# Soft mixture-of-experts layer: the combination's steps pinned a tile apart, column variances, single turn pieces, two tiles combined early

## The chip, the cores and the metric

The kernel runs on one core of one Trainium2 chip. A core has five engines that run beside each other, each with its own instruction queue: TensorE (PE, matrix products and transposes into PSUM banks), VectorE (DVE), ScalarE (ACT), GpSimd (POOL) and SyncE (SP, which here issues nearly all DMAs). The metric is the device time of one execution in microseconds (us); lower is better. All values are float32 unless a trace line says otherwise.

## The reference

The input is 4096 rows of 256 values. Four residual blocks follow each other, each behind a LayerNorm:

```
x = x + attention_a(layernorm(x))      # 16 heads of 16, causal, softmax with an extra term in its sum
x = x + softmoe(layernorm(x))
x = x + attention_b(layernorm(x))      # 16 heads of 16, causal
x = x + softmoe(layernorm(x))
```

The change is in the soft mixture of experts, which is (64 experts of 32 slots, so 2048 columns):

```
logits  = (x @ phi_w.T + phi_b).reshape(4096, 64, 32)
D       = softmax(logits, over the 32 slots)
C       = softmax(logits, over the 64 experts)
Xt      = D^T x                         # 2048 x 256: every slot's mixture of the rows
Xt      = tanh(layernorm(clip(Xt, -33000, 65000)))
Yt      = Xt[expert] @ expert_w[expert] + expert_b[expert]
out     = C Yt                          # 4096 x 256
```

## The kernel before

Rows are cut into 32 tiles of 128 (`NT`), and `x` stays in SBUF. The program runs attention a, the first expert layer, attention b and the second expert layer. An expert layer (`_Experts.run`) has three sweeps over the 32 tiles and a transition.

**First and second sweep** (`h` = 0 and 1: the first and the second 1024 of the 2048 columns). `logits(h, t)` makes 128×1024 logits on PE (tile `lg`), adds the bias on DVE (L775), stores the result to a DRAM tile `ld[t]` for later, takes the maximum per expert on DVE (L780), subtracts it on POOL (L783), takes the exponential on ACT (L786), and keeps the maximum over experts in `cm` (L787, DVE). `divide(h, t)` sums on DVE (L796), inverts (L797) and multiplies on POOL (L798): that is D. PE then adds Dᵀx into four PSUM banks `acc` (four calls of 512 columns per tile). Logits run two tiles ahead of the accumulation, and division one tile ahead.

**Pieces beside.** `net.side` is a queue of small pieces; `net.beside(3)` takes one. After each accumulation two are taken in the first sweep and one in the second. In the first sweep the pieces come from `norm_pieces`: row statistics, scaling, and two turns for every four tiles. A turn transposes two tiles of `x` on PE (L70) into the `bank` of the pool `psm`, which holds one bank, and ACT copies it to `xnT` (L753). The first eight tiles are normed and turned ahead of the sweep. In the second sweep the pieces are the LayerNorm of the first half of X̃ (which stands transposed, features in partitions) and its expert products: `centre` (mean by a matmul with a constant matrix, subtraction on DVE, square on POOL L693), `spread` (variance by a matmul with the same matrix, so repeated over all 128 partitions; square root on ACT L701; reciprocal of 128×512 on DVE L702), `squash` (multiplication on POOL L707, tanh on ACT L708), and eight `product`s (PE, then a bias add on DVE L720).

**Transition.** The second half of X̃ goes through the same steps. Between them stand the first tile's turn and the first half of its combination. Combination of tiles 0 and 1 begins at the end of the second sweep.

**Third sweep** (the combination, C Ỹ). `combine_begin(t)` loads the 128×2048 logits (1 MB) and the residual rows `xl`, takes `mc`, the larger of the two halves' `cm`, on DVE (L811), subtracts it on POOL in two halves (L815) and takes exponentials on ACT (L818). `combine_sums(t)` reduces over the experts on DVE (L824), inverts (L825) and repeats the 32 sums four times by a POOL copy, `s4` (L827). `turn(t)` transposes that to `rT` on PE, copies it to `r` on ACT (L835), makes 16 transposes of 128×128 in groups of four into `ps` (four PSUM banks), and multiplies each group by `r` into `lT` on DVE (L842). `weigh(t)` is 16 matmuls into `o` and a residual add on DVE (L860); in the first layer row statistics follow (`net.stats`, L94 and L95), in the second the store. Step `t` of the loop writes `combine_begin(t+2)`, `turn(t+1)`, `combine_sums(t+2)` and `weigh(t)`. In the first layer, the first pieces of attention b are taken in this loop from tile 6 on.

**The order.** A tile scheduler orders each engine's instructions by its own costs. Exempt are those under `keep_in_program_order`, which stay in the order they are written: before, that holds for PE's matmuls and transposes alone (`net.mm`, L66, and `net.tr`, L69). Where a pool has fewer buffers than the program has open tiles of it, the next write waits for the last reader.

Of the kernel before, what the change touches and what calls it, by code (L numbers as in the profile page):

```python
# [19 lines left out]
P = 128  # L20
# [586 lines left out]
class _Experts:  # L607
# [8 lines left out]
    def __init__(self, net, phiT, phi_b, ew, eb, out=None, attention=None):  # L616
        self.net, self.phiT, self.phi_b = net, phiT, phi_b
        self.ew, self.eb, self.out = ew, eb, out
        self.attention = attention
        self.phi = net.zone[:, 0 : 2 * E].rearrange("p (c e) -> p c e", c=2)  # L620
        self.phb = net.zone[:, 2 * E : 3 * E]

    def load(self):
        nc, EH = self.net.nc, E // 2
        for h in range(2):
            for c in range(2):
                nc.sync.dma_start(
                    self.phi[:, c, ts(h, EH)], self.phiT[ts(c, P), ts(h, EH)]
                )
# [5 lines left out]
    def run(self):  # L635
# [10 lines left out]
        with ExitStack() as ctx:  # L646
# [4 lines left out]
            sp = pool("ff_s", 4)  # L651
            net.banks = pool("psm", 1, space=PSUM)
# [3 lines left out]
            nc.gpsimd.memset(mean, 1.0 / D)  # L656
            ys = [cp.tile([P, NC2, D], F32, name="ys0"), None]
# [8 lines left out]

            def load_w(ec, w=None):
                if w is None:
                    w = ewp.tile([P, 4, 2, D], F32, name="w")
                nc.sync.dma_start(w, ew[ts(ec, 4)].rearrange("n (c p) h -> p n c h", p=P))  # L670
                ews[ec] = w

            def load_b(h):
                b = rp.tile([P, NC2, D], F32, name="ebt")
                for j in range(4):
                    nc.sync.dma_start(
# [5 lines left out]

            sqs = {}

            def centre(n):
# [4 lines left out]
                sq = ewk.tile([P, 2, 512], F32, name="sq")  # L690
                for d in range(2):
                    nc.vector.tensor_tensor(xs[:, d, :], xs[:, d, :], mu, ALU.subtract)
                    nc.gpsimd.tensor_tensor(sq[:, d, :], xs[:, d, :], xs[:, d, :], ALU.mult)  # L693
                sqs[n] = sq

            def spread(n):
                sq = sqs[n]
                var = net.bank()
                for d in range(2):
                    mm(var, mean, sq[:, d, :], start=d == 0, stop=d == 1)  # L700
                nc.scalar.activation(sq[:, 0, :], var, AF.Sqrt, bias=net.eps)  # L701
                nc.vector.reciprocal(sq[:, 0, :], sq[:, 0, :])  # L702

            def squash(n):
                xs = xt[:, :, ts(n, 512)]
                for d in range(2):
                    nc.gpsimd.tensor_tensor(xs[:, d, :], xs[:, d, :], sqs[n][:, 0, :], ALU.mult)  # L707
                nc.scalar.activation(xs, xs, AF.Tanh)  # L708

            def product(ec):  # L710
                w = ews.pop(ec)
                y = net.bank()[:, 0:D]
# [20 lines left out]
            def norm_pieces(j):  # L733
                def stats(i2):
                    for t in (4 * j + 2 * i2, 4 * j + 2 * i2 + 1):
                        net.stats(t)
                    if i2:
                        net.roots(4 * j, 4 * j + 4)

                def scale():  # L740
                    for t in range(4 * j, 4 * j + 4):
                        nc.scalar.activation(
                            x[:, t, :], x[:, t, :], AF.Identity,
                            bias=shift[:, t : t + 1], scale=rstd[:, t : t + 1],
                        )

                def turn(i2):
                    t2 = 2 * j + i2
                    pt = net.bank().rearrange("p (c i t) -> p c i t", c=2, i=2)
                    for i in range(2):  # L750
                        for c in range(2):
                            tr(pt[:, c, i, :], x[:, 2 * t2 + i, ts(c, P)])
                    nc.scalar.copy(  # L753
                        xnT[:, :, ts(t2, 2 * P)], pt.rearrange("p c i t -> p c (i t)")
                    )

                return [
                    lambda: stats(0), lambda: stats(1), scale, lambda: None,
                    lambda: turn(0), lambda: turn(1),
                ]  # L760
# [4 lines left out]
            def logits(h, t):  # L765
                l = lp.tile([P, NH, SLOT], F32, name="l")
                lf = l.rearrange("p n s -> p (n s)")
                for n in range(2):
                    lg = pl.tile([P, 512], F32, name="lg")
                    for c in range(2):  # L770
                        mm(
                            lg, xnT[:, c, ts(t, P)], phi[:, c, ds(h * EH + n * 512, 512)],
# [5 lines left out]
                nc.sync.dma_start(ld[t][:, h, :], lf)  # L778
# [22 lines left out]
            ce, css, lTs, xls, pools = {}, {}, {}, {}, {}  # L801

            def combine_begin(t):
                l = pools["l"].tile([P, NEXP, SLOT], F32, name="l")
                nc.sync.dma_start(
                    l.rearrange("p n s -> p (n s)"), ld[t].rearrange("p h e -> p (h e)")
                )
                xl = sp.tile([P, D], F32, name="xl")
                nc.sync.dma_start(xl, xd[:, t, :])
                m = sp.tile([P, SLOT], F32, name="mc")  # L810
                nc.vector.tensor_tensor(m, cm[:, t, 0, :], cm[:, t, 1, :], ALU.max)  # L811
                e = pools["e"].tile([P, NEXP, SLOT], F32, name="e")
                for h in range(2):
                    ns = ts(h, NH)
                    nc.gpsimd.tensor_tensor(  # L815
                        e[:, ns, :], l[:, ns, :], _bc(m.unsqueeze(1), [P, NH, SLOT]), ALU.subtract
                    )
                    nc.scalar.activation(e[:, ns, :], e[:, ns, :], AF.Exp)  # L818
                ce[t], xls[t] = e, xl


            def combine_sums(t):
                s = sp.tile([P, SLOT], F32, name="sc")
                nc.vector.tensor_reduce(s, ce[t].rearrange("p n s -> p s n"), AX.X, ALU.add)  # L824
                nc.vector.reciprocal(s, s)  # L825
# [241 lines left out]
```

## Time and profile before

| | us |
|---|---|
| three runs | 5325.7, 5330.68, 5327.17 |
| median | 5327.17 |
| the profiled execution | 5322.71 |
| its span, first to last instruction | 5321.0 |
| first layer: first sweep, second sweep | 276.4, 241.8 |
| first layer: transition, third sweep (tiles 2 to 31) | 75.0, 297.8 |
| second layer: first sweep, second sweep | 276.5, 242.2 |
| second layer: transition, third sweep (tiles 2 to 31) | 74.9, 295.3 |

| engine | busy us | share of the span |
|---|---|---|
| PE | 5025.3 | 94% |
| DVE | 4142.4 | 78% |
| ACT | 2608.9 | 49% |
| POOL | 1208.7 | 23% |

The stages were cut by the trace: a sweep runs from its first logits or transposes to the end of its last accumulation, the transition from there to the first matmul of `weigh(2)`. In the lines of a trace, `o<-ys,lT` names the output tile and the inputs of an instruction, `128*128 128x512` the contraction and the output of a matmul; a float32 matmul appears as several records. `[9.59 <-POOL s L827]` behind an instruction is the idle time of its engine before it and what ended it. In the rows by group the columns are busy time, mean nanoseconds of one, and idle time with its releasers. PEclk is the granted TensorE clock, 1.00 being full speed; PE's busy time is partly modelled.

### The profile page before, as it was taken

How to read it: one execution, taken by the hardware profiler on the slowest of the kernel's cores; microseconds unless marked ns; L12 is line 12 of the kernel's file. 1: busy time of each engine (PE TensorE's matmuls, PEld its weight loads, DVE VectorE, ACT ScalarE, POOL GpSimd, SP SyncE). 2: the span in 40 equal slices, each digit the busy share in tenths (PEclk: the TensorE clock that was granted, in tenths of full speed). 3: DMA queues.
4: the chain of work that ended last, by engine and by line, in shares of the span. 5: the costliest groups of instructions: out<-in, count | busy, mean ns of one | idle time of the engine just before them, and what ended most of it. 6: DMA issues, size and time to landing. Idle time of an engine off the chain costs nothing.

```text
span 5321.0 us, 79263 instructions
## 1 busy us (share of the span) xinstructions
PE 5025.3 (94%) x29824; PEld 2663.5 (50%) x29824; DVE 4142.4 (78%) x7742; ACT 2608.9 (49%) x3036; POOL 1208.7 (23%) x1178
## 2 busy tenths in 40 slices
PE   7999999999999899979989999999999998999799
PEld 4444454545454344447744454444454543444577
DVE  5788998989987478767757888989899864787665
ACT  3566666666677412122235666666666674111221
POOL 3211000000000345454411110000000003455443
PEclk9999999999999999989989999999999999999899
DMA  6433221222211211443353342222222112113432
GB/s 248 140 111 121 74 68 63 69 63 63 62 59 42 85 68 67 138 142 113 119 199 130 105 128 68 66 70 61 63 63 67 56 36 86 67 75 135 143 129 90
DMA packets 265584, 499.16 MB, mean 94 GB/s; under 512 B 44880, under 2 KB 109904, under 8 KB 257008
## 3 DMA queue, kind: packets, MB, share of 16 engines
q1 hardware_dynamic: 259968, 485.57, 27.5%
q10 hardware_dynamic: 4896, 7.87, 0.4%
q8 instruction: 234, 3.83, 0.3%
q14 instruction: 150, 1.23, 0.1%
q0 software_dynamic: 336, 0.66, 0.0%
HBM read 336.73 MB, written 156.76 MB: 93 GB/s over the span
## 4 chain that ended last, share of the span: by engine, by line
PE 65%; DVE 14%; POOL 11%; ACT 4%; issue 4%; DMA 1%; SPq 0%; DVEq 0%; POOLq 0%; ACTq 0%
PE bank L67 20%; PE o L67 20%; PE sc L67 17%; POOL e L815 5%; DVE mx L386 4%; DVE sc L824 4%; PE lg L67 3%; POOL e L783 3%; PE acc L67 3%; DVE junk L380 2%; POOL e L798 2%; ACT e L786 2%; DVE l L775 1%; ACT e L818 1%; ACT pb L462 1%
## 5 line engine op out<-in xcount | busy, mean ns | idle before, releaser
L462 ACT ACTIVATE pb<-sc 128x1024 f32<-128x1024 f32 (+3 forms) x2304 | 2071.0, 951 | 1093.2 <-PE sc L67 1090.3
L386 DVE TENSOR_REDUCE mx<-bank 128x1 f32<-128x512 f32 x3584 | 2223.2, 681 | 169.9 <-PE bank L67 165.7
L67 PE MATMUL bank<-k,q 64*128 64x512 f32 (+3 forms) x4608 | 1350.0, 452 | 72.8 <-DVE mx L386 29.9
L67 PEld LDWEIGHTS bank<-k,q 64*128 64x128 f32 x4608 | 666.5, 185 | 1178.6 <-DVE mx L386 780.3
L67 PE MATMUL o<-pb,va 128*32 128x512 f32 (+3 forms) x9216 | 1158.2, 574 | 0.9 <-POOL pb L466 0.7
L67 PE MATMUL sc<-q,k 64*128 64x512 f32 (+3 forms) x4608 | 988.1, 390 | 9.9 <-ACT pb L462 9.4
L67 PE MATMUL sc<-qm,one 64*128 64x512 f32 (+3 forms) x4608 | 946.9, 376 | 0.0
L466 POOL TENSOR_SCALAR_AFFINE_SELECT pb<-pb 128x256 f32<-128x256 f32 x512 | 205.7, 408 | 2260.5 <-ACT pb L462 2254.8
L380 DVE CUSTOM_DVE_ANT_0 junk<-bank,maskw 128x128 bf16<-128x128 f32 (+3 forms) x1024 | 501.6, 490 | 259.1 <-PE bank L67 151.8
L67 PEld LDWEIGHTS sc<-q,k 64*128 64x128 f32 x4608 | 508.8, 186 | 138.4 <-ACT pb L462 99.8
L67 PEld LDWEIGHTS sc<-qm,one 64*128 64x128 f32 x4608 | 525.6, 186 | 66.6
L786 ACT ACTIVATE e<-e 128x1024 f32<-128x1024 f32 x128 | 135.2, 1056 | 786.3 <-POOL e L783 786.3
L67 PE MATMUL acc<-e,x 128*128 128x512 f32 x1024 | 472.1, 605 | 35.2 <-POOL e L798 33.6
L67 PE MATMUL lg<-zone,xnT 128*128 128x512 f32 x1024 | 469.3, 602 | 0.2
L67 PE MATMUL o<-ys,lT 128*128 128x256 f32 x2048 | 453.0, 379 | 0.0
L67 PEld LDWEIGHTS o<-ys,lT 128*128 128x128 f32 x2048 | 384.5, 190 | 51.8 <-issue 2.0
L818 ACT ACTIVATE e<-e 128x1024 f32<-128x1024 f32 x128 | 135.3, 1057 | 459.3 <-POOL e L815 449.6
L67 PEld LDWEIGHTS acc<-e,x 128*128 128x128 f32 x1024 | 197.9, 194 | 290.5 <-issue 242.4
L798 POOL TENSOR_TENSOR e<-e,s 128x1024 f32<-128x1024 f32 x128 | 244.7, 1913 | 385.7 <-DVE s L797 385.7
L67 PEld LDWEIGHTS o<-pb,va 128*32 128x32 f32 x9216 | 182.9, 108 | 285.8 <-issue 263.2
L67 PEld LDWEIGHTS lg<-zone,xnT 128*128 128x128 f32 x1024 | 194.9, 193 | 242.5 <-issue 229.5
L815 POOL TENSOR_TENSOR e<-l,mc 128x1024 f32<-128x1024 f32 x128 | 299.6, 2363 | 24.1 <-DVE x L860 17.1
(101 smaller groups left out, 3234.9 us busy)
## 6 DMA issues: line engine op xcount, KB each, us to landing
k<-ak SPq DMA_DIRECT2D x144, 512.0 KB
k<-bk SPq DMA_DIRECT2D x144, 512.0 KB
ld<-l SPq DMA_DIRECT2D x128, 512.0 KB
l<-ld SPq DMA_DIRECT2D x64, 1024.0 KB
w<-in_L_ffn_expert_w_dram SPq DMA_DIRECT2D x24, 1024.0 KB
q<-aq SPq DMA_DIRECT2D x32, 512.0 KB
rb<-dd SPq DMA_DIRECT2D x64, 256.0 KB
q<-bq SPq DMA_DIRECT2D x32, 512.0 KB
```

The costliest lines, as they stand in the source:

```text
L67: self.tc.keep_in_program_order(self.nc.tensor.matmul(*a, **k))
L380: nc.vector.tensor_tensor_reduce(out=junk[:, 0:w], in0=scs[h2][:, 0:w], in1=maskw[:, QB - w : QB], scale=1.0, scalar=-3e38, op0=ALU.add, o ...
L386: nc.vector.tensor_reduce(m, scs[h2], AX.X, ALU.max)
L462: nc.scalar.activation(pb[:, :, off:QB], sc[:, :, off:QB], AF.Exp)
L466: nc.gpsimd.affine_select(out=d, in_=d, compare_op=ALU.is_ge, fill=0.0, base=0, pattern=[[0, 2], [1, P]], channel_multiplier=-1,)
L775: nc.vector.tensor_tensor(lf[:, ts(n, 512)], lg, phb[:, ds(h * EH + n * 512, 512)], ALU.add)
L783: nc.gpsimd.tensor_tensor(e, l, _bc(m.unsqueeze(2), [P, NH, SLOT]), ALU.subtract)
L786: nc.scalar.activation(ef, ef, AF.Exp)
L798: nc.gpsimd.tensor_tensor(e, e, _bc(s.unsqueeze(2), [P, NH, SLOT]), ALU.mult)
L815: nc.gpsimd.tensor_tensor(e[:, ns, :], l[:, ns, :], _bc(m.unsqueeze(1), [P, NH, SLOT]), ALU.subtract)
L818: nc.scalar.activation(e[:, ns, :], e[:, ns, :], AF.Exp)
L824: nc.vector.tensor_reduce(s, ce[t].rearrange("p n s -> p s n"), AX.X, ALU.add)
```

## The change

- `phi` is laid out with the halves of the columns outermost, so that each half lies together in the zone; tile 0's early exponentials and the last loads of weights are written over the parts no longer read.
- Every DMA of the layer on SP is pinned to its written order (`dma`), and the DVE and ACT steps of the combination too (`pin`).
- `centre` squares on ACT in one operation. `spread` makes the variances as columns: eight one-column matmuls, root and reciprocal of 128×4, and a product of the identity with them on DVE. `squash` turns that diagonal back to rows by one matmul with ones, and multiplies on DVE from PSUM.
- The norm of a group of four tiles is one piece (`norm`), and each turn is a piece of its own (`turn_x`). The first two turns are written to `lg` banks. In the first sweep one piece is taken before the accumulation and one after it; in the second, one before it.
- The combination is split: `maxima`, `load_l`, `begin`, `sums` (or `quarter` four times), `turn_r`, `turn`, `weigh`, `ended`. In step `t` of the third sweep stand `load_l(t+4)`, `ended(t-1)`, `begin(t+3)`, `turn(t+1)`, `maxima(t+4)`, `sums(t+2)`, `weigh(t)`, `turn_r(t+2)`. The copy `s4` is on ACT. `ps` has three banks, and products of the transition alternate between two.
- Tiles 0 and 1 begin in the second sweep: subtractions and exponentials by halves at steps 14, 16, 18 and 20, sums by quarters at 21 to 28, and their turns ahead of the last two accumulations. Tile 2 begins there too, and its sums are taken by quarters between the transition's products.
- Attention b's first pieces start one tile later (6 and 10 instead of 5 and 9).

The diff, cut to its core:

```diff
+        self.phi = net.zone[:, 0 : 2 * E].rearrange("p (h c e) -> p h c e", h=2, c=2)
...
+            pin = tc.keep_in_program_order
+            def dma(o, i):
+                pin(nc.sync.dma_start(o, i))
...
-                sq = ewk.tile([P, 2, 512], F32, name="sq")
                 for d in range(2):
                     nc.vector.tensor_tensor(xs[:, d, :], xs[:, d, :], mu, ALU.subtract)
-                    nc.gpsimd.tensor_tensor(sq[:, d, :], xs[:, d, :], xs[:, d, :], ALU.mult)
-                sqs[n] = sq
+                sqs[n] = ewk.tile([P, 2, 512], F32, name="sq")
+                nc.scalar.activation(sqs[n], xs, AF.Square)
             def spread(n):
                 sq = sqs[n]
                 var = net.bank()
-                for d in range(2):
-                    mm(var, mean, sq[:, d, :], start=d == 0, stop=d == 1)
-                nc.scalar.activation(sq[:, 0, :], var, AF.Sqrt, bias=net.eps)
-                nc.vector.reciprocal(sq[:, 0, :], sq[:, 0, :])
+                for k in range(4):
+                    for d in range(2):
+                        mm(
+                            var[:, k : k + 1], sq[:, d, ts(k, P)], mean[:, 0:1],
+                            start=d == 0, stop=d == 1,
+                        )
+                r = sp.tile([P, 4], F32, name="rx")
+                nc.scalar.activation(r, var[:, 0:4], AF.Sqrt, bias=net.eps)
+                nc.vector.reciprocal(r, r)
+                nc.vector.tensor_tensor(
+                    sq[:, 0, :].rearrange("p (k e) -> p k e", k=4),
+                    _bc(net.ident.unsqueeze(1), [P, 4, P]), _bc(r.unsqueeze(2), [P, 4, P]),
+                    ALU.mult,
+                )
             def squash(n):
                 xs = xt[:, :, ts(n, 512)]
+                rs = net.bank()
+                mm(rs, one, sqs[n][:, 0, :], start=True, stop=True)
                 for d in range(2):
-                    nc.gpsimd.tensor_tensor(xs[:, d, :], xs[:, d, :], sqs[n][:, 0, :], ALU.mult)
+                    nc.vector.tensor_tensor(xs[:, d, :], xs[:, d, :], rs, ALU.mult)
                 nc.scalar.activation(xs, xs, AF.Tanh)
...
+            def maxima(t):
+                cms[t] = sp.tile([P, SLOT], F32, name="mc")
+                pin(nc.vector.tensor_tensor(cms[t], cm[:, t, 0, :], cm[:, t, 1, :], ALU.max))
+            def load_l(t):
+                cl[t] = pools["l"].tile([P, NEXP, SLOT], F32, name="l")
+                dma(cl[t].rearrange("p n s -> p (n s)"), ld[t].rearrange("p h e -> p (h e)"))
+                xls[t] = xlp.tile([P, D], F32, name="xl")
+                dma(xls[t], xd[:, t, :])
+            def exponentials(t, l, h):
+                ns, e = ts(h, NH), ce[t]
+                nc.gpsimd.tensor_tensor(
+                    e[:, ns, :], l, _bc(cms[t].unsqueeze(1), [P, NH, SLOT]), ALU.subtract
                 )
...
+                pin(nc.scalar.activation(e[:, ns, :], e[:, ns, :], AF.Exp))
+            def begin(t):
+                ce[t] = pools["e"].tile([P, NEXP, SLOT], F32, name="e")
+                l = cl.pop(t)
                 for h in range(2):
...
+                    exponentials(t, l[:, ts(h, NH), :], h)
+            def inverse(t, s):
+                pin(nc.vector.reciprocal(s, s))
+                css[t] = sp.tile([P, 4, SLOT], F32, name="s4")
+                pin(nc.scalar.copy(css[t], _bc(s.unsqueeze(1), [P, 4, SLOT])))
+            def sums(t):
                 s = sp.tile([P, SLOT], F32, name="sc")
...
+                pin(nc.vector.tensor_reduce(
+                    s, ce[t].rearrange("p n s -> p s n"), AX.X, ALU.add
+                ))
+                inverse(t, s)
+            sqp = {}
+            def quarter(t, k):
+                if k == 0:
+                    sqp[t] = sp.tile([P, 4, SLOT], F32, name="sq4", bufs=2)
+                pin(nc.vector.tensor_reduce(
+                    sqp[t][:, k, :], ce[t][:, ts(k, NEXP // 4), :].rearrange("p n s -> p s n"),
+                    AX.X, ALU.add,
+                ))
+                if k == 3:
+                    s = sp.tile([P, SLOT], F32, name="sc")
+                    pin(nc.vector.tensor_reduce(
+                        s, sqp.pop(t).rearrange("p k s -> p s k"), AX.X, ALU.add
+                    ))
+                    inverse(t, s)
+            def turn_r(t, bank=None):
+                rT = (bank or (lambda: pools["r"].tile([P, 512], F32, name="rT")))()[:, 0:P]
                 tr(rT, css.pop(t).rearrange("p j s -> p (j s)"))
...
+                rts[t] = sp.tile([P, P], F32, name="r")
+                pin(nc.scalar.copy(rts[t], rT))
+            def turn(t, bank=None):
+                r = rts.pop(t)
                 e = ce.pop(t).rearrange("p n s -> p (n s)")
                 lT = pools["lT"].tile([P, NEC, P], F32, name="lT")
                 for e4 in range(NEC // 4):
...
+                    ps = (bank or (lambda: pools["t"].tile([P, 512], F32, name="ps")))()
+                    ps = ps.rearrange("p (i t) -> p i t", i=4)
                     for i in range(4):
                         tr(ps[:, i, :], e[:, ts(4 * e4 + i, P)])
...
+                    pin(nc.vector.tensor_tensor(
                         lT[:, ts(e4, 4), :], ps, _bc(r.unsqueeze(1), [P, 4, P]), ALU.mult
...
+                    ))
                 lTs[t] = lT
...
+            def ended(t):
+                pin(nc.vector.tensor_tensor(x[:, t, :], os.pop(t), xls.pop(t), ALU.add))
...
+            first = lambda: pl.tile([P, 512], F32, name="lg")
+            norm(0)
+            norm(1)
+            turn_x(0, first)
+            turn_x(1, first)
+            for j in range(2, NT // 2):
+                if j % 2 == 0 and j > 2:
+                    net.side.append(lambda j=j: norm(j // 2))
+                net.side.append(lambda j=j: turn_x(j))
             seq = [(h, t) for h in range(2) for t in range(NT)]
...
+            def early(t, h):
+                if h == 0:
+                    maxima(t)
+                    ce[t] = z(0, E) if t == 0 else rp.tile(
+                        [P, NC2, D], F32, name="ebt"
+                    ).rearrange("p c (n s) -> p (c n) s", s=SLOT)
+                    xls[t] = xlp.tile([P, D], F32, name="xl")
+                    dma(xls[t], xd[:, t, :])
+                l = z(2 * E, EH)
+                dma(l.rearrange("p n s -> p (n s)"), ld[t][:, h, :])
+                exponentials(t, l, h)
+            ahead = {}
+            for k in range(4):
+                ahead[14 + 2 * k] = lambda k=k: early(k // 2, k % 2)
+            for k in range(8):
+                ahead[21 + k] = lambda k=k: quarter(k // 4, k % 4)
+            ahead[29] = lambda: [maxima(t) for t in range(2, 4)]
...
+                if n < len(seq) - 2:
+                    net.beside(3)
+                else:
+                    assert not net.side and not net.urgent and not net.agenda
+                if h == 1 and t in ahead:
+                    ahead[t]()
                 if n == len(seq) - 2:
                     nctx.close()
-                    pools["e"] = pool("fc_w", 2)
+                    pools["lT"] = pool("fc_t", 2)
                     pools["l"] = pool("fc_l", 1)
-                    pools["lT"] = pool("fc_t", 1)
+                    pools["e"] = pool("fc_w", 1)
+                    load_l(2)
+                    turn_r(0, first)
+                    turn(0, first)
+                    begin(2)
...
+                    load_l(3)
+                if n == len(seq) - 1:
+                    turn_r(1, first)
+                    turn(1, first)
+                    load_b(1)
...
+                if h == 0:
+                    net.beside(3)
...
+            pools["e"] = pool("fc_w1", 1)
             pools["r"] = pool("fc_r", 1, space=PSUM)
-            pools["t"] = pool("fc_p", 4, space=PSUM)
+            pools["t"] = pool("fc_p", 3, space=PSUM)
             pools["o"] = pool("fc_o", 2, space=PSUM)
+            two = pool("fc_x", 1, space=PSUM)
+            weigh(0, 0, NC2)
             centre(2)
             centre(3)
-            turn(0)
             spread(2)
             spread(3)
-            weigh(0, 0, NC2)
+            weigh(1, 0, NC2)
             squash(2)
             squash(3)
             for ec in range(NC2, NEC):
-                product(ec)
-                if ec == NC2:
-                    load_w(NEC - 1)
+                product(ec, (net.bank, lambda: two.tile([P, 512], F32, name="bank2"))[ec % 2])
+                if ec < NC2 + 2:
+                    load_w(ec + 6)
+                if ec < NC2 + 4:
+                    quarter(2, ec - NC2)
+            turn_r(2)
+            begin(3)
...
             for t in range(NT):
-                if t + 2 < NT:
-                    combine_begin(t + 2)
+                if t + 4 < NT:
+                    load_l(t + 4)
+                if t > 0:
+                    ended(t - 1)
+                    if t + 3 < NT:
+                        begin(t + 3)
                 if t == 0:
                     weigh(0, NC2, NEC)
-                if t + 1 < NT:
+                if 2 <= t + 1 < NT:
                     turn(t + 1)
-                if t + 2 < NT:
-                    combine_sums(t + 2)
+                if t > 0 and out is None:
+                    net.stats(t - 1)
+                if t + 4 < NT:
+                    maxima(t + 4)
+                if 4 <= t + 2 < NT:
+                    sums(t + 2)
                 if t > 0:
-                    weigh(t, 0, NEC)
+                    weigh(t, NC2 if t == 1 else 0, NEC)
+                if 4 <= t + 2 < NT:
+                    turn_r(t + 2)
+                if t == 0:
+                    sums(3)
+                    turn_r(3)
...
-                    if t in (5, 9):
-                        b = (t - 5) // 4
+                    if t in (6, 10):
+                        b = (t - 6) // 4
...
-                    if t > 5:
+                    if t > 6:
                         net.beside(3)
+            ended(NT - 1)
```

## The prediction

> **What bounds the kernel now.** I read the chain first, for the engine at the end of the work.
>
> ```profile
> PE 65%; DVE 14%; POOL 11%; ACT 4%; issue 4%; DMA 1%; SPq 0%; DVEq 0%; POOLq 0%; ACTq 0%
> ```
>
> The attention sections (all before 1780 us and 2671 to 4428 us) issue the same instructions in both kernels, so I cut the rest into stages: busy times for each layer's first sweep, second sweep, transition (last accumulation to `weigh(2)`) and third sweep.
>
> ```profile
> core 0: us, PE busy (x) PEld busy (x) DVE busy (x) ACT busy (x) POOL busy (x), PEclk, DMA share, GB/s
> 1780.20:2056.60 276.40, 252.39 (x624) 115.49 (x623) 201.99 (x223) 50.14 (x58) 131.71 (x80) 0.98 0.24 88
> 2056.60:2298.40 241.80, 229.65 (x628) 98.81 (x627) 187.21 (x201) 40.32 (x38) 124.77 (x69) 0.98 0.36 125
> 2298.40:2373.40 75.00, 42.74 (x278) 29.90 (x276) 46.23 (x44) 19.81 (x22) 39.47 (x25) 0.84 0.37 125
> 2373.40:2671.20 297.80, 284.82 (x1475) 236.81 (x1474) 212.40 (x294) 74.96 (x104) 128.96 (x80) 1.00 0.34 116
> ...
> 4947.20:5022.10 74.90, 42.80 (x277) 29.96 (x277) 45.79 (x43) 19.81 (x22) 37.97 (x24) 0.84 0.33 114
> 5022.10:5317.40 295.30, 276.19 (x1438) 230.40 (x1436) 189.89 (x224) 59.49 (x80) 128.83 (x80) 1.00 0.33 113
> ```
>
> First-layer sweeps leave PE idle 24 and 12 us; the transition 32, at a clock of 0.84. The third sweep looks PE-bound, but busy PE there is partly a modelled wait. Its chain shows the real period:
>
> ```profile
> 5102.46 3.71 DVE sc L824
> ...
> 5106.20 0.36 DVE sc L825
> ...
> 5106.68 0.05 POOL s L827
> ...
> 5106.93 4.69 POOL e L815 x2
> ...
> 5111.64 1.06 ACT e L818
> ...
> 5112.73 3.71 DVE sc L824
> ```
>
> This repeats every 10.27 us: POOL's small copy L827 queues between one tile's subtractions and the next's, so subtractions, exponentials and sums of neighbouring tiles cannot overlap. At the end, where tiles are ready in advance, outputs come 8.76 to 8.80 us apart (6.91 for `weigh`, 1.86 for the turn): PE's own need.
>
> **First sweep.** Both turns of a pair use the one `bank`, so the second waits for ACT's copy, which stands behind an exponential:
>
> ```profile
> L70 PE MATMUL bank<-ident,x 128*128 128x128 f32 x128 | 21.2, 290 | 32.0 <-ACT xnT L753 32.0
> ```
>
> The change puts the turns in separate pieces and the first two in other banks: −16 per layer. One more saved at the start (5.1 us of transposes and copies through one bank). Two attention-output projections that stood together are now apart: −2.5 (the second waited 2.47). Against this, POOL's loop through subtraction, exponential, sum and multiply takes 7.125 us where PE needs 6.87; PE's stalls hid that. Over some 20 tiles 0.255 each shows: +5. Sum −14; bounds −18 (POOL's pace hidden) and −8 (half of the turn waits return as waits for the copy).
>
> **Second sweep, norm of X̃.** The slow steps are these (transition rows; the sweep's own are alike):
>
> ```profile
> L702 DVE RECIPROCAL sq<-sq 128x512 f32<-128x512 f32 x2 | 6.5, 3293 | 0.0
> L707 POOL TENSOR_TENSOR xt<-xt,sq 128x512 f32<-128x512 f32 x4 | 5.0, 1265 | 3.7 <-DVE sq L702 3.7
> ```
>
> Two 3.3-us reciprocals and four POOL multiplies delay POOL's normal multiply, and the accumulations stand 14.06 and 10.49 us apart where 6.87 would do. With variances as columns the reciprocal has 4 columns (L825 with 32 takes 0.35), the diagonal is one DVE multiply of 512 elements (at most 0.7), the way back one 0.85-us matmul, and the scaling four DVE operations of 0.68 (as L692). The square's one ACT operation of 1024 elements costs 1.06, off the path. The fourteen steps that carry these pieces and the products now take 8.58 + 8.85 + 8.79 + 8.58 + 7.66 + 14.06 + 10.49 + 7×8.08 = 124; I get 2×8.58 + 2×8.7 + 2×7.7 + 8×8.09 + 3 of stalls left = 118: −6, between 0 and −9.
>
> **Second sweep, early tiles.** Subtractions and exponentials of tiles 0 and 1 fit in POOL's 3.3-us idle stretch between subtraction and multiply, so they cost about 1. The quarter sums do not: 3.71/4 = 0.93 of DVE stands between reciprocal and second logit add, on the 7.125 loop. With 0.26 of slack used up already, eight cost some 0.83 each: 6.6, and two closing sums and reciprocals with the maxima 1.2: +8.8. Reloading `l` by halves is SP work with free bandwidth (DMA share 0.36); bounds: 3 (DVE's slack absorbs most) to 14 (each early piece costs its whole duration). Turns of tiles 0 and 1 before the last two accumulations add 3.7 of PE time, partly under waits of 2.17 and 2.96 there: +3.4. Sweep net: −6 + 8.8 + 3.4 ≈ +6, from −2 to +14.
>
> **Transition.** Before, 75. Now PE has: means 3.4, first halves of `weigh(0)` and `weigh(1)` 6.9, variances 3.6, broadcasts 1.7, products 8×1.3 = 10.4 (two banks; 1.67 each now), second halves 6.9, turn(2) and two small ones 2.5: 35.4. Uncovered: clips of the last sums 2.8; scaling, table load (1.28) and tanh to the first product 6; the copy of r behind an exponential before `turn_r(3)` 3.5; pool changes 1.5. Together 49.2: −26, bounds −30 and −15 (the square, sqrt and reciprocal in a row, still uncovered, are the low bound's).
>
> Here the clock matters. In before, PE resumes after `[9.59 <-POOL s L827]` and 16 transposes take 3.4 us, where the chain's steady 16 take 1.75. The Trainium skill ("TensorE: Matmul & The Clock Gate", HAM oscillation) says that idle stretches beyond about 3.4 us bring the slow clock back; by it my 6 and 3.5 would each still cost some 2 us, and the transition would be 53. I keep 49: my stretches are bounded above by less than the 9.59 seen.
>
> **Third sweep.** Now the copy `s4` goes to ACT, subtractions run a tile ahead (`begin(t+3)` beside `weigh(t)`), sums of t+2 and turns of t+1 follow in a pinned order. POOL needs 4.7 a tile, ACT 2×1.06 + 2×0.3, DVE x 0.36, lT 4×0.62 (0.68 with the pipeline's start), mc 0.19, sc 3.71, reciprocal 0.36: 7.1 to 7.4. PE's 8.77 is the bound. What is queued behind each wait: with three `ps` banks instead of four, the turn's last four transposes wait for the first lT, which waits for `ended(t-1)`'s add: about 0.23. So 9.0 × 30 = 270 in the second layer against 295.3: −25 (bounds −27 and −5).
>
> In the first layer ACT, in about eight tiles by the built order, copies r only behind the next tile's two exponentials, and in some five separate places PE then waits 1.9 to 2.6: +12. Attention pieces make eight tiles longer: 22×9.13 + 4×9.5 + 4×10.5 = 281. One more piece is left over after the last tile: +2.4. Sum 295.4 against 297.8: −2 (bounds −14 and +12).
>
> **Sum.** 2×(−14 + 6 − 26) − 25 − 2 = −95. The profiled execution took 5322.71 at a span of 5321.0; span 5226, execution 5228. It lies 4.5 under the median of 5327.17, so the forecast is 5232. A measurement of this kernel can tell about 0.2%, 10.7 us, from no change (its three runs spread over 5).
>
> **Rivals.**
> Cleaner (0.13): the r copies never come late, the first layer's third sweep gains like the second's (−15 to −25), early work is absorbed: −120, 5207. For: ACT is 25% busy there. Against: the built order.
>
> The third sweep keeps its period (0.14). The row
>
> ```profile
> L811 DVE TENSOR_TENSOR mc<-cm 128x32 f32<-128x32 f32 x19 | 3.7, 193 | 46.3 <-POOL e L815 46.3
> ```
>
> shows mc starting only when both subtractions of POOL have ended, 2.43 later than it could. The change pins mc(t+4) ahead of the sums of t+2. If mc waits for POOL itself, and not for a buffer's last reader, DVE's tile becomes 7.3 + 2.4 = 9.75: 30 tiles 293, about −2 in the second layer and nothing in the first. Then the sweeps' −68 are all: 5257. Against: the lT multiplies, with one SBUF input, show no such wait. The Trainium skill ("SBUF — State Buffer", Who interferes with whom) speaks for it: a DVE instruction with two SBUF inputs is locked out while a GpSimd one reads SBUF. The waits of 2.43 agree, though a buffer's release would look alike; by that rule the time is this rival's 5257.
>
> Slower: lockstep on the fourth turn bank (0.09). With three banks PE stands until DVE frees the first. If DVE is then still inside its 3.71 reduction, PE waits it out in every tile: 8.77 + 3.7 = 12.5, 375 per third sweep, +157 for both, less 68: +89, 5416. It decides where DVE's 7.1 to 7.4 of a tile, begun when `weigh(t-1)` ends, are not done as `weigh(t)` ends, 8.77 later. Slack is 1.4, less what hand-offs take, and statistics of the first layer (0.4) come out of it; I see no more than 0.5 of hand-offs in the chain above, which speaks against.
>
> The change does not do what it says (0.04): turns still share one bank after the first two, and if ACT's copies stay behind exponentials, all stage gains fall to their low bounds: 2×(−8 + 14 − 15) = −18, and the third sweeps 0 with the extra 2.4 and 12 of the first layer: −4, no change.
>
> **How the numbers follow.** The forecast has 0.60. Faster: 0.60 + 0.13 (cleaner) + 0.14 (period kept) = 0.87; same 0.04; slower 0.09. The range starts at 5195, below the cleaner rival's 5207, since the sweeps' upper bounds would take another 12, and ends at 5300: 5257 and most of the 2×(6 + 8 + 11) = 50 between the stages' values and their low bounds. Outside remain the lockstep, the no-change case and some 0.05 of tails.
>
> **What would show it.** Right: third-sweep outputs 9.0 apart in the second layer, with PE's idle time a fraction of a microsecond before the fourth `ps` group; first-layer ones 9.1, with a few of 11 where r comes late; transition near 49 at a clock above 0.9; L702's successor under 0.4; no idle time before the sweep's turns; accumulations 7.0 to 7.2 apart in the first sweep and about 8 where quarter sums run. Wrong: outputs at 9.7 or more with mc waiting for POOL; PE waiting 3 or more for lT; sweep 2 over 256; a transition still over 60.

## The result, and the profile after

The changed kernel takes 5242.3 us (median of 4 runs, 5236.0 to 5251.4) against 5328.5 for the kernel before: ratio 0.9840, 95% interval 0.9823 to 0.9857. Measured once more later: 5235.8 (5 runs) against 5327.6, ratio 0.9824 (0.9810 to 0.9837). The forecast was 5232, range 5195 to 5300.

The page's chain (the work that ended last, followed back), after the change:

```profile
PE 75%; DVE 11%; POOL 5%; issue 3%; ACT 3%; DMA 2%; SPq 0%; DVEq 0%; POOLq 0%; ACTq 0%
```

POOL fell from 11% of the chain to 5%. Windows by stage, same columns as before (first sweep, second sweep, transition and third sweep of the first layer, then the second layer's last two):

```profile
1793.50:2039.12 245.62, 240.61 (x609) 110.55 (x610) 192.79 (x211) 48.99 (x57) 128.02 (x79) 0.99 0.20 78
2039.12:2296.18 257.06, 244.10 (x702) 107.42 (x701) 206.86 (x239) 49.60 (x51) 133.97 (x69) 0.97 0.44 145
2296.18:2350.27 54.09, 41.08 (x271) 29.32 (x271) 24.33 (x42) 12.36 (x16) 12.81 (x6) 0.91 0.35 107
2350.27:2654.06 303.79, 281.39 (x1471) 242.05 (x1470) 218.59 (x294) 83.31 (x132) 124.59 (x54) 0.98 0.34 116
...
4915.30:4971.00 55.70, 42.47 (x271) 31.34 (x271) 23.84 (x40) 13.63 (x17) 12.90 (x6) 0.88 0.31 91
4971.00:5236.05 265.05, 265.05 (x1438) 232.39 (x1436) 201.78 (x226) 71.80 (x109) 123.15 (x53) 1.00 0.40 132
```

For the comparison I cut all traces at the same events: the start of attention's last copy `ot`, the last accumulation of each sweep, the first matmul of `weigh(2)`, the last of `weigh`. (This puts the sweeps' border 6.7 us earlier than the prediction's windows did.) Microseconds, first layer / second layer:

| stage | before | after | after again | difference | forecast |
|---|---|---|---|---|---|
| attention a | 1780.3 | 1793.5 | 1787.7 | +13.2 | 0 |
| first sweep | 269.6 / 269.3 | 245.6 / 244.6 | 245.1 / 244.5 | −24.0 / −24.7 | −14 |
| second sweep | 248.5 / 248.5 | 257.1 / 258.4 | 257.1 / 257.9 | +8.5 / +9.9 | +6 |
| transition | 75.0 / 74.9 | 54.1 / 55.7 | 55.8 / 58.2 | −20.9 / −19.2 | −26 |
| third sweep | 297.8 / 295.3 | 303.8 / 265.1 | 305.5 / 265.0 | +6.0 / −30.3 | −2 / −25 |
| attention b | 1758.2 | 1758.2 | 1761.9 | 0 | 0 |

The changed stages give −94.7, where −95 was forecast; but single terms are off by up to 11, in both directions. Attention a, whose instructions did not change, lost 13.2 in this profile, so the profile's span fell by 81.7 only (5321.0 to 5239.3). The second layer's third sweep is now PE alone, 8.97 a tile (the chain, three of its steps):

```profile
5112.58 0.11 PE rT L70
5112.69 1.95 PE ps L70 x16
5114.64 6.91 PE o L67 x32
```

### The profile page after: what moved, and what is told of

It reads as the page before. It is cut to its first block, busy times and chain, and to the rows that moved or that the text cites. A ratio compares the mean times of both kernels' runs of the same rounds, so it can differ in the third digit from the quotient of the medians.

```text
span 5239.3 us, 79442 instructions
## 1 busy us (share of the span) xinstructions
PE 5025.7 (96%) x29936; PEld 2683.4 (51%) x29936; DVE 4141.6 (79%) x7790; ACT 2633.1 (50%) x3108; POOL 1157.2 (22%) x1084
## 4 chain that ended last, share of the span: by engine, by line
PE 75%; DVE 11%; POOL 5%; issue 3%; ACT 3%; DMA 2%; SPq 0%; DVEq 0%; POOLq 0%; ACTq 0%
PE o L67 26%; PE bank L67 22%; PE sc L67 17%; PE acc L67 4%; DVE mx L386 4%; PE lg L67 4%; DVE junk L380 2%; POOL e L794 2%; PE ps L70 2%; POOL e L809 2%; ACT e L797 1%; DVE l L786 1%; ACT pb L462 1%; POOL e L826 1%; DMA zone<-ld 0%
## 5 line engine op out<-in xcount | busy, mean ns | idle before, releaser
L797 ACT ACTIVATE e<-e 128x1024 f32<-128x1024 f32 x128 | 135.2, 1057 | 694.6 <-POOL e L794 694.6
L67 PE MATMUL o<-ys,lT 128*128 128x256 f32 x2048 | 464.9, 386 | 1.6 <-DVE xt L985 1.6
L826 POOL TENSOR_TENSOR e<-l,mc 128x1024 f32<-128x1024 f32 x120 | 281.3, 2365 | 319.5 <-DMA l<-ld 209.9
L807 DVE TENSOR_REDUCE s<-e 128x32 f32<-128x1024 f32 x128 | 156.1, 1219 | 155.2 <-ACT e L797 154.6
```

The source lines that it names most:

```text
L67: self.tc.keep_in_program_order(self.nc.tensor.matmul(*a, **k))
L797: nc.scalar.activation(ef, ef, AF.Exp)
L807: nc.vector.tensor_reduce(s, e, AX.X, ALU.add)
L826: nc.gpsimd.tensor_tensor(e[:, ns, :], l, _bc(cms[t].unsqueeze(1), [P, NH, SLOT]), ALU.subtract)
```

## The experiments

**What opened the third sweep's loop.** First the kernel before with one line changed:

```diff
-                nc.gpsimd.tensor_copy(s4, _bc(s.unsqueeze(1), [P, 4, SLOT]))
+                nc.scalar.copy(s4, _bc(s.unsqueeze(1), [P, 4, SLOT]))
```

> The kernel before with one line changed: the copy s4 (L827) runs on ACT instead of POOL. Nothing is pinned and no tile starts early. Theory 1 (the loop is closed by POOL's copy): without it POOL's subtractions run ahead, PE's 8.77 us a tile is the bound, outputs of the third sweep come 8.8 to 9.1 apart in the second layer (270 us instead of 295 for tiles 2 to 31), some 275 to 285 instead of 298 in the first, and the transition loses part of its waits for this copy (75 to between 60 and 72): 5265 to 5285 in all. Rival (the steps must be a tile apart and pinned): subtraction, exponential, sum and copy of a tile still follow each other, the outputs stay over 10 apart, and the time is within 10 of 5328.

Measured: 5266.8 us, ratio 0.9895 (0.9875 to 0.9915); third sweeps 269.7 and 259.4, transitions 77.2 and 78.1. Theory 1 held for the third sweep, not for the transition. Its chain in the second layer:

```profile
5111.38 0.11 PE rT L70
5111.48 1.75 PE ps L70 x16
5113.23 6.91 PE o L67 x32
```

That is 8.77 a tile, PE's own need, with nothing pinned but PE's order, as before. One line does more for the third sweeps (−28 and −36) than all of the change does (+6 and −30).

Then the reverse, the changed kernel with that copy back on POOL:

```diff
-                pin(nc.scalar.copy(css[t], _bc(s.unsqueeze(1), [P, 4, SLOT])))
+                nc.gpsimd.tensor_copy(css[t], _bc(s.unsqueeze(1), [P, 4, SLOT]))
```

> The changed kernel with the copy s4 back on POOL, all else as changed. In the built order the copy stands between the subtractions of two tiles. Theory 1: the old loop returns (subtractions 4.69, exponential 1.06, sums 3.71, reciprocal 0.36, hand-offs 0.45), outputs 10.2 to 10.4 apart, 300 to 308 us for the second layer's third sweep instead of 265, and the kernel at 5305 to 5325 although every step is a tile apart. Rival (pinning and distance do it): a tile of distance hides the copy, outputs stay at 9.0 to 9.4, the kernel at 5240 to 5255.

Measured: 5248.3, ratio 0.9851 (0.9833 to 0.9870); third sweeps 308.8 and 269.4, outputs 9.17 apart in the second layer. Here the rival was right. The group rows (window 5000 to 5200) show how:

```profile
L841 POOL COPY s<-sc 128x128 f32<-128x128 f32 x21 | 6.1, 289 | 88.8 <-DVE sc L839 88.8
...
L70 PEld LDWEIGHTS rT<-ident,s 128*128 128x128 f32 x22 | 3.1, 139 | 7.3 <-POOL s L841 7.2
```

POOL still stands 88.8/21 = 4.2 us a tile behind the sum, but PE waits only 7.2/22 = 0.33. The copy of tile t+2 now stands between the subtractions of t+3 and t+4, so the old loop no longer closes from one tile to the next. Another loop does, and it has no exponential in it:

```profile
5064.57 4.69 POOL L826 TENSOR_TENSOR e<-l,mc 128x1024 f32<-128x1024 f32 x2
```

```profile
5067.94 1.37 DVE L816 TENSOR_TENSOR mc<-cm 128x32 f32<-128x32 f32 x1
5069.23 3.73 DVE L845 TENSOR_REDUCE sc<-e 128x32 f32<-128x2048 f32 x1
```

`mc`, which takes 0.19 elsewhere, ends at 5069.31, when POOL's two subtractions end (5069.26). The sum pinned behind it takes 3.73 and the reciprocal 0.35; then comes POOL's copy, at 5073.48, and with it the next subtractions: 9.16 from copy to copy (5064.32 to 5073.48), which is the 9.17 of the outputs. So each edit opens the old loop: the copy taken off POOL, or subtractions a tile ahead with the pins that the change brings.

**The norm's turns alone**, in the kernel before (edit: `norm_pieces` replaced by `norm` and `turn_x` as in the change's diff, pieces taken as there).

> The kernel before with the norm's turns alone as in the change: single pieces, the first two in the banks of the logits, one piece before the accumulation and one after it. Theory: the first sweep falls from 269.5 to about 245.5 us (from the end of attention a's last copy to the last accumulation), as in the changed kernel, so 48 in all: 5280. Rival: part of the 24 comes from the pinned DMAs and the layout of phi; then 253 or more, 5297 or more.

Measured: 5285.1, ratio 0.9917 (0.9902 to 0.9932); first sweeps 244.6 and 245.5, second sweeps 2.6 and 2.9 longer, transitions 76.6, or 1.6 longer, the third sweeps as they were. The whole 24 is the turns'. Before, PE idled 32.0 at these transposes, both layers together; in the changed kernel their rows wait for nothing:

```profile
L70 PE MATMUL bank<-ident,x 128*128 128x128 f32 x112 | 16.8, 273 | 0.0
```

**The norm of X̃ alone**, in the kernel before (edit: `centre`, `spread` and `squash` as in the change's diff).

> The kernel before with the norm of Xt alone as in the change: squares on ACT, variances as columns, the way back by a matmul, scaling on DVE. Theory: the steps of the second sweep that carry it fall by 9 us (124 to 115), and the transition by 8 to 12 of its 75, since its two reciprocals of 3.3 us and POOL's multiplies stand on its path: 34 to 42 in all, 5286 to 5294. Rival: the transition is set by the combination of tiles 0 and 1 on POOL, and only the sweep gains: 18, 5310.

Measured: 5316.0, ratio 0.9981 (0.9971 to 0.9990); second sweeps 240.1 and 239.6 (−8.5 and −8.9), transitions 76.6 and 76.5 (+1.6, as with the turns alone, so not a price of the columns). The rival was right. In the transition PE idles 5.73 us before `rT` of a tile, behind POOL's copy `s4`:

```profile
2308.82 0.47 PE L70 MATMUL rT<-ident,s 128*128 128x128 f32 x1 [5.73 <-POOL s L842]
```

That copy itself waits 5.23 for DVE's sum of 3.7, and after the idle stretch the granted clock is 0.50 until 2325. So the combination's steps set this stage, and shorter steps of the norm beside them gain nothing.

**The three small edits together**, on the kernel before.

> The kernel before with three small edits together: s4 copied on ACT, the norm's turns as in the change, the norm of Xt as in the change. Nothing pinned, nothing early, four ps banks. Theory (the stages add): third sweeps 270 and 259 as with the s4 edit alone, first sweeps 245, second 240 plus 2.6, transitions about 77: 120 below the kernel before, 5208 us, so some 30 below the whole change. Rival (they share ACT or DVE, so they do not add): the s4 copies and squares on ACT delay exponentials, and it stays at 5230 to 5245.

Measured: 5205.1, ratio 0.9767 (0.9753 to 0.9782). They add: first sweeps 245.4, second 241.4 and 242.7, transitions 75.7 and 74.2, third sweeps 269.7 and 259.4. This is below the whole change, whose interval (0.9810 to 0.9857 over both measurements) does not reach it.

**Why the first layer's third sweep got longer.** In the changed kernel's timeline at its start:

```profile
2357.15 0.30 ACT L841 COPY s<-sc 128x128 f32<-128x128 f32 x1 [3.05 <-DVE sc L839]
2357.35 1.06 ACT L829 ACTIVATE e<-e 128x1024 f32<-128x1024 f32 x1
...
2357.50 0.33 PE L70 MATMUL rT<-ident,s 128*128 128x128 f32 x1 [0.16 <-ACT s L841]
...
2359.25 1.06 ACT L829 ACTIVATE e<-e 128x1024 f32<-128x1024 f32 x1 [0.83 <-POOL e L826]
2360.21 0.25 ACT L872 COPY r<-rT 128x128 f32<-128x128 f32 x1
...
2361.24 1.02 PE L70 MATMUL ps<-ident,e 128*128 128x128 f32 x4 [2.03 <-DVE lT L884]
```

`rT` is there at 2357.8, but its copy stands on ACT behind an exponential that waits for POOL; lT and the fourth group of transposes follow late. A pinned instruction is tied to the one written before it on its engine. In the first layer that is often one of attention b's, which is not pinned itself and moves, so the chain is cut. The edit ties the exponentials to the last r:

```diff
-                pin(nc.scalar.copy(rts[t], rT))
+                lastr[0] = nc.scalar.copy(rts[t], rT)
+                pin(lastr[0])
...
-                        begin(t + 3)
+                        with tc.issue_after(lastr[0].ins):
+                            begin(t + 3)
```

> The changed kernel, with the exponentials of tile t+3 issued on ACT behind the copy r of the tile before them (only the order on ACT changes, and only in the first layer). Theory: in the first layer attention b's own ACT instructions break the pinned chain, r stands behind the next tile's exponentials, and PE waits for lT; with r ahead the first layer's third sweep falls from 304 to 285 to 290 us, and nothing else moves: 5223 to 5228. Rival (POOL waits for the loads of l there, and exponentials come late whatever the order): 298 or more, 5236 or more.

Measured: 5215.4, ratio 0.9785 (0.9770 to 0.9799); the first layer's third sweep 282.5 (−21.3), the other changed stages within 3. The theory held, and more was in it than expected.

**Three banks or four** (edit: `fc_p` with 4 banks; `bank2` replaced by a tile of `pools["r"]`).

> The changed kernel with four ps banks instead of three; the transition's products take turns with the bank of rT in place of a bank of their own. Theory: PE stops waiting for the first lT, outputs of the second layer come 8.77 instead of 8.97 apart: 259 us instead of 265, 6 less in the first layer too, the transitions as they were: 5230. Rival (the 0.2 is the wait for r behind the new tile's add, whatever the banks): 8.97 stays, 5242.

Measured: 5210.9, ratio 0.9770 (0.9753 to 0.9786); outputs of the second layer 8.77 apart in most tiles (262.3), the first layer 281.5. So the 0.2 was the bank. The first layer gained 22 without any change of order: with four banks all transposes of a tile run before lT is needed, so part of what a late r costs comes through the missing bank. Not all of it: with four banks and r first together (the version of all that was learned, below) that sweep takes 271.5, another 10 less.

**The second sweep's end.** The step that turns tile 0 took 14.64 in the changed kernel:

```profile
2276.01 2.11 PE L70 MATMUL lg<-ident,zone 128*128 128x128 f32 x8 [2.34 <-DVE l L786]
2281.56 1.12 PE L70 MATMUL lg<-ident,zone 128*128 128x128 f32 x4 [3.44 <-ACT r L872]
```

> The changed kernel with two moves in the second sweep. The small transposes of the early tiles' sums are written at steps 27 and 28, so that their copies r stand ahead of tile 31's exponential on ACT and not behind it; tile 0 begins at steps 3 and 5 and its quarter sums are at steps 9 to 12, beside products. Theory: the step of 14.6 falls to 9 or 10, since PE waited there for lT behind r; the four quarters hide under products (8.09 a step anyway), where now they make steps of 7.97 out of 6.87: 9 to 10 per layer, 5222 to 5226. Rival (DVE is full in the product steps too): the steps at 9 to 12 become 9.0, and only the 5 of the late r are gained: 5232.

Measured: 5238.5, ratio 0.9832 (0.9817 to 0.9847); second sweeps 259.9 and 257.9. The quarter sums at steps 9 to 12 cost nothing (steps of 8.09 with and without them). But the small transposes took one of three logit banks and kept it until r was copied, and the second also waited for its `s4`, 11.21 of idle PE: one step of 20.84. A miss, by where r's transposes were put.

**Attention a.**

> The changed kernel once more, unchanged. Theory: attention a, whose instructions are the same in every kernel, took 1780 to 1794 us in the profiles so far; the 13 us that the changed kernel's profile lost there are not its own, so another profile lies anywhere in that interval, the stages after it agree within 2 us with the first profile's, and the ratio to the kernel before is 0.982 to 0.985. Rival (its own): 1792 to 1795 again.

Measured: 5235.8, ratio above; attention a 1787.7. Of the other stages the second layer's transition (58.2 for 55.7) and attention b (1761.9 for 1758.2) differ by more than the 2 expected, so a difference of 2 in one transition says little. Over the profiles of all kernels, with the same instructions there, it took 1780.3 to 1794.2, and the first profile of before has the lowest value. The windows 100 to 400 us of before and after:

```profile
100.00:200.00 100.00, 90.77 (x562) 45.31 (x561) 68.38 (x207) 45.62 (x66) 34.93 (x55) 0.91 0.39 126
200.00:400.00 200.00, 193.32 (x1285) 98.06 (x1283) 163.96 (x405) 117.00 (x149) 33.27 (x61) 1.00 0.36 118
```

```profile
100.00:200.00 100.00, 89.58 (x525) 44.92 (x522) 63.99 (x189) 42.34 (x61) 33.00 (x53) 0.83 0.38 124
200.00:400.00 200.00, 193.06 (x1250) 97.71 (x1250) 159.37 (x398) 114.48 (x145) 33.64 (x60) 0.97 0.34 114
```

The clock comes up later in one than in the other, and most of the 13 us (9.4 by 394 us) is lost here.

**A version of all that was learned**: four banks, r first, tile 0's early steps beside products, r's transposes in the norm's bank.

> The changed kernel with four ps banks, the exponentials behind r in the first layer, tile 0 begun at steps 3 and 5 with its quarter sums at 9 to 12, tile 1 at 17 and 19 with quarters at 21 to 24, and the small transposes of both at steps 26 and 28 into the norm's bank, idle then, so that no bank of the logits waits for r. Theory: third sweeps about 272 and 260 (8.77 a tile), second sweeps 247 to 249 instead of 257 (four quarters hidden: 4; no wait of 5 for r in the step before the last), first sweeps and transitions as in the change: 5180 to 5190, below the three small edits' 5205. Rival (the wait before the last accumulations is the logit banks' own, freed by additions that stand behind the exponential's sum): second sweeps stay at 252 or more, 5192 to 5200.

Measured: 5190.3, ratio 0.9745 (0.9731 to 0.9758). Third sweeps 271.5 and 260.7 as expected; second sweeps 253.9 and 254.8, the rival's. A step of 14.9 is left:

```profile
2279.29 1.12 PE L70 MATMUL lg<-ident,zone 128*128 128x128 f32 x4 [5.92 <-DVE lT L887]
```

The pinned lT stands on DVE behind tile 31's sum, and an accumulation that is ready behind the turn on PE. So the turn of tile 0 went behind that accumulation, tile 1's into the transition:

> The version before this one (four banks, r first, early tiles moved) with the turns of tiles 0 and 1 moved once more: tile 0's behind the accumulation of tile 30 and not ahead of it, tile 1's and the load of the biases into the transition behind the second mean. Theory: in the profile so far PE waits 5.9 us there for the fourth group's bank, freed by an lT multiply that stands on DVE behind tile 31's sum; the accumulation of tile 30, ready 8 us earlier, is queued behind that. Moved, the second sweep falls from 254 to 246 to 248, the transition keeps its 55 to 57 (the turn fills waits there): 12 to 16 in all, 5175 to 5180. Rival (the wait moves with the turn): accumulation 31 and the transition lose what accumulation 30 gains, and the two stages together stay at 309 to 310, 5190.

Measured: 5199.4, ratio 0.9754 (0.9738 to 0.9770). Neither theory: PE idled 9.56 before the turn for a weight load, which I had left written ahead of the turn and into tile 0's exponentials. It combined other values for tile 0. With the loads behind it:

> a_last with the loads of the last three weights and of tile 3's logits written behind tile 0's turn. In a_last they were written ahead of it, into the part of the zone that holds tile 0's exponentials, so the turn waited for the load, 9.6 us of idle PE, and took weights for exponentials. Theory: that wait goes, the second sweep is at 247 to 250 instead of 254 in a_final, the transition at 55 to 58, as long as the weights still land before their products: 5176 to 5184. Rival (the loads, now later, are late for the products): the transition grows to 60 or more, 5190.

Measured: 5176.5 (5 runs), ratio 0.9715 (0.9702 to 0.9729), the fastest: second sweeps 249.2 and 248.6, transitions 53.8 and 54.8, third sweeps 272.7 and 259.5.

## Why the prediction was right, and where it was not

**First sweep, −24 for −14.** The turns' stall was right in place, too small in size, and the +5 for POOL's pace was wrong. Of the 24.0, 3.5 lies ahead of the end of the first accumulation, where 1 was forecast, and 20.4 between that and the last one, where 18.5 less the 5 was forecast. Accumulations in the changed kernel are 6.87 apart from step 12 to 28. The loop of 7.125 that I read in the second sweep's end shows only in the last two (7.06 and 7.13); before that nothing is held to it.

**Second sweep.** The norm gave 8.5 to 8.9 alone (forecast 6: the stalls left were under 3). The early tiles' sums cost 7.3 in the first layer (seven steps of 7.16 to 8.47, each less 6.87) and 9.8 in the second, forecast 8.8. The turns ahead of the last accumulations were mis-sized: from the third last accumulation to the end of the last it is 14.64 + 8.08 + 3.60 = 26.3 in the first layer, where before it was 5.76 + 6.66 + 5.25 = 17.7: +8.7 for +3.4. I had charged PE's time and left out that r and lT, pinned, queue behind tile 31's exponential and sum. The clock has a part in it too: from 2276, after the wait of 2.34 shown above, the granted clock was 0.50 for 13.7 us, and the second last accumulation took 6.19 where an undisturbed one takes 3.60 to 3.70, so some 2.5 of the 8.7.

```profile
2276.00:2289.70 13.70, 9.34 (x23) 5.16 (x24) 7.97 (x12) 3.32 (x4) 10.35 (x5) 0.50 0.88 290
```

```profile
2284.50 6.19 PE L67 MATMUL acc<-e,x 128*128 128x512 f32 x8
```

**Transition, −20 for −26.** The sum missed the clock. I argued that stretches of idle PE below the 9.59 of before would not bring it down. They did, and the transitions' granted clock was 0.91 and 0.88:

```profile
2302.00:2306.00 4.00, 2.38 (x5) 0.68 (x4) 1.49 (x3) 1.06 (x1) 0.00 (x0) 1.00 0.00 0
2306.00:2310.00 4.00, 2.11 (x18) 2.06 (x18) 1.26 (x3) 2.60 (x3) 0.00 (x0) 1.00 0.00 0
2310.00:2313.00 3.00, 3.00 (x17) 3.00 (x16) 0.69 (x1) 0.00 (x0) 0.00 (x0) 0.53 0.02 5
2313.00:2319.00 6.00, 6.00 (x19) 4.67 (x18) 0.87 (x2) 0.26 (x1) 0.00 (x0) 0.67 0.00 0
```

The second variance took 3.26 where the first took 1.92, the half of `weigh(1)` 5.71 where that of `weigh(0)` took 3.72: 3.3 of the miss. The last product's wait for its weights (2.17, a DMA) is another part, and so are the first three products, which took 4.51 with the clock at 0.50 from 2324 to 2327, where three later ones took 3 × 1.09. The wait before `turn_r(3)` was 3.18, forecast 3.5. That the column variances alone save nothing here was not in the forecast. What they save once tiles 0 and 1 begin early was not measured apart.

**Third sweep.** Second layer: 8.97 for 9.0, and the 0.2 is the fourth bank's, as four banks showed. It gained 5 more than forecast because I multiplied 9.0 by 30: 28 tiles are 8.97 apart, and the last two take 6.91 and 7.07. First layer: the term for late r copies was 12 and is 21.3; the rest was right (282.5 without it, 281 forecast). I had counted five separate places in the built order; ten tiles are 1.4 to 4.2 longer than the 9.14 that they take with r first.

**Rivals.** The lockstep did not come: PE waited 21.5 in all for lT in the first layer's third sweep, and by its rows 0.0 in the second's (the 0.2 a tile stands inside the busy time of its transposes there, 1.95 for 1.75). One of the waits was 4.3, though, behind a late r, and a wait of 3 or more for lT is what the prediction named as a sign of being wrong; the others were 2.1 at most. The period was not kept, although mc is held by POOL: with `s4` on ACT the sums rarely wait for that, and with `s4` on POOL this rival's mechanism sets the 9.17. Another sign, "sweep 2 over 256", did not come: by the prediction's border that is 14 above the kernel before, and the second sweeps grew by 8.5 and 9.9.

**Sum.** −94.7 for −95, by luck of opposite errors; the stages and their causes were mostly right, the sizes were not: the transitions (5 and 7 short), the second sweeps (3 and 4 over) and the first layer's third (8 over) stand against the first sweeps (10 and 11 more than forecast) and the second layer's third (5 more).

## What to carry to other kernels

Before rebuilding an order, take the cheapest link out of the loop that the chain shows and measure: one line gave the third sweeps all that PE allows, and three small edits beat the whole change. A pin ties an instruction to the one written before it on its engine, and through a chain of pins to all before that, whether or not it needs them; the chain is cut by any unpinned neighbour; count what stands ahead of each pinned step. A spare bank hides part of what late operands cost.

## What the runs showed of the hardware

**The clock falls without a long idle stretch.** Ahead of the half clock at 2310, PE's longest idle stretch was 1.47 us; ahead of the one at 2276 it was 2.34. The Trainium skill ("TensorE: Matmul & The Clock Gate", HAM oscillation) puts the limit at idle gaps above about 3.4 us. No gap in these records is that long. Nor does the longer gap decide: after a wait of 3.18 the clock stayed at 1.00.

```profile
2342.82 0.33 PE L70 MATMUL rT<-ident,s 128*128 128x128 f32 x1 [3.18 <-ACT s L841]
```

```profile
2340.00:2344.00 4.00, 1.18 (x11) 1.18 (x12) 3.89 (x7) 0.96 (x3) 2.79 (x2) 1.00 0.09 27
2344.00:2350.00 6.00, 6.00 (x39) 5.17 (x38) 3.50 (x7) 1.72 (x2) 3.58 (x2) 1.00 0.56 190
```

The share of busy time alone does not order these cases either: PE was busy 1.18 of 4 there, and 2.38 and 2.11 of two windows of 4 ahead of the half clock at 2310. The latter is nearly all one-column matmuls (1.92). Whether these count as idle (then the stretch at 2310 is longer than the limit, though the one at 2276 is not), or whether a low share must last for longer, no run here separates.

**A DVE instruction with two SBUF inputs is held while POOL runs.** In the changed kernel with `s4` on POOL, `mc` takes 1.37 us in the median tile of the second layer, where before it took 0.19, and it ends with POOL's subtractions (its lines stand with that experiment). In the version with r in the norm's bank, two mc of 0.2 us took 1.74, and ended 0.14 after POOL's multiply of 1.91. The time lies inside mc's record, with no wait ahead of it, so it is not a buffer's. This agrees with the Trainium skill ("SBUF — State Buffer", Who interferes with whom). In the changed kernel it costs little: mc takes 0.30 on average over all tiles, and in the second layer's third sweep POOL is idle for 111.6 of 258 us. The kernel before shows the same delay as idle time ahead of mc (46.3 over 19); why it stands outside the record there is open.
